# Cross attention on one core: the order of outputs, copies, statistics and last sums

## The chip, the cores and the metric

The kernel runs on one core of one Trainium2 chip. The metric is the device time of one execution in microseconds (us): 1736.73 us before the change, the median of three runs (1733.67 to 1740.61). The core's engines work side by side, each through a queue of its own in program order, and wait for each other on semaphores. TensorE (PE, with its weight loads as PEld) multiplies, VectorE (DVE) and ScalarE (ACT) evict, transpose and exponentiate, GpSimd (POOL) does small products and additions. DMAs are issued from the queues of ScalarE, POOL and SyncE (SP).

## The reference, cut to what matters

A decoder of four layers over x of shape (8, 56, 256): each layer is a self attention, a cross attention and a feed-forward block, each followed by a residual addition and a normalisation. The change touches the cross attentions of layers 0, 2 and 3, over a context `kv_c` of 1500 rows of 64 columns per batch element. They have 16 heads and differ in their weights (layer 3 leaves out the rotation of the queries):

```python
q_r = einsum("bshq,hqr->bhsr", q_big, W_qr)
k_r = einsum("bld,hdr->bhlr", kv_r, W_kr)        # kv_r: the rotated context
scores = einsum("bhsr,bhlr->bhsl", q_r, k_r)
attn = softmax(scores, axis=-1)
ctx_c = einsum("bhsl,bld->bhsd", attn, kv_r)
ctx_lat = einsum("bhsd,hkd->bhsk", ctx_c, w_kc_kv)
return ctx_lat.transpose(0, 2, 1, 3).reshape(B, S, H * K) @ Wo.T
...
x = layernorm(x + xattn(x, ctx_512, ...), axis=-1)
```

## The kernel before

The 448 rows of x lie as four tiles of 112 (`NT`, two batch elements each). `x_queries` folds the query weights so that a head's query against the context has 64 values; they lie in `qa`, on partitions 0 to 63 and again on 64 to 127. The two last projections are folded as well: per head `w_kc_kv` times `Wo` gives 64 x 256 numbers of `wm`. wm is made in four quarters of four heads by `weighted` (eight multiplications into columns 384 to 511 of the four banks `acc`, then one copy to `wm`).

`x_tiles` does the rest for the 8 batch elements. A batch has 16 x 56 = 896 queries, in 7 tiles of 128. One pass of the loop is a step n, for tile i = n mod 7 of batch b = n div 7; there are 56 steps. For a tile, `scored` multiplies 128 queries with 1500 keys into the four banks `sc4`, in two halves u; `moved` evicts each half on VectorE and keeps the row minimum of the negated scores; `weights` exponentiates on ScalarE and sums the rows; `turned` transposes 32 x 32 blocks on VectorE into `cells`. One batch later, in steps i = 0 to 5, `gather` multiplies the transposed weights with the context rows `kv`, into columns 0 to 223 of `acc`. `cells` is one buffer: the transposes of one batch write over what the sums of the batch before it have read, so a transpose of step i = 1 must wait for the sums of step i = 0.

The other parts of a batch are set into steps of the next ones. `inverted` takes the reciprocals of the row sums and puts them on diagonals (POOL); `spread` multiplies these with ones, so that each inverse stands on 64 partitions, in columns 256 to 383 of `acc`; `spread_out` copies them to `rec`. `halves_of(0)` at i = 5 and `halves_of(1)` at i = 6 copy the sums to `num` and `other`; `placed` adds the two and multiplies with the inverse on POOL into `qa`, whose first columns are free by then. `output` multiplies these with wm at i = 6, half a tile of rows (four of the eight pairs of heads) at a time, again into columns 384 to 511 of `acc`; `joined` copies that and adds it to X. In the first three batches, where there is nothing to output, step i = 6 has `weighted` in that place: quarters 2 and 3 in steps 13 and 20. Quarters 0 and 1 are made in steps 4 and 5, where no sums exist yet. `measured` takes mean and variance of a finished tile of X on VectorE: tiles 0 and 1 at i = 2 of batches 5 and 7, tile 2 behind the loop.

Every instruction of `x_tiles` goes through `do`, that is `ordered` (L361 to L374; the profile shows L365 for all of them). It binds each instruction to the one before it on its engine, so the queues keep the order in which the lines are written. The context rows of a batch come in thirds, four DMAs each, from ScalarE's queue (`rows_of`), the keys from POOL's queue (`columns`).

In the last step (n = 55) both halves of tile 2 are put out and joined. What is behind the loop (L1040 to L1066) is called the end here: the inverses of the last batch, its sums into `sc4`, the statistics and normalisation of tiles 0 to 2, the transposes of their rows (`turn_x`), the additions of the last sums' halves (`twin`, `last`) and the products with the inverse (`inv`) on VectorE, then the last tile's multiplication with wm, its addition, normalisation and transposes.

## Time and profile before

| | |
|---|---|
| median of three runs | 1736.73 us |
| profiled execution | 1739.46 us, span 1737.2 us |
| mean granted TensorE clock | 0.905 |
| PE, DVE, ACT, POOL busy | 1541.5, 1092.3, 622.5, 323.5 us |
| 168 exponentials on ACT | 1544 ns each |
| 168 transposes on DVE | 1766 ns each |
| evictions of a half on DVE | 935 and 958 ns |
| copies of a quarter of wm on ACT | 12, 585 ns each |
| copies of half an output (`y`) on ACT | 18, 372 ns each |
| the loops and ends of the three cross attentions | near 229 to 462, 878 to 1114, 1422 to 1657 us |

A line of the timeline reads: start in us from the span's start, duration in us, engine, source line, operation, output<-input, shapes (partitions x elements), count; in brackets the idle time of the engine just before and what ended it. A row can hold several instructions that follow each other. TensorE's fp32 multiplications show as two records each, so eight of them are x16. The view of busy time by window has, after the engines, the granted TensorE clock (1.00 is full), the busy share of the DMA engines and GB/s.

### The profile page before, as it was taken

The numbers are of one execution on the slowest core, as the hardware profiler recorded it, in microseconds if no ns is written. First come the engines' busy times: TensorE is split into PE (matmuls) and PEld (weight loads), VectorE is DVE, ScalarE is ACT, GpSimd is POOL, SyncE is SP. The second block draws the span as 40 slices with busy tenths as digits, with TensorE's granted clock in tenths as the row PEclk, the third lists the DMA queues.
The fourth block names the chain that finished last, engine by engine and source line by source line (L and its number), as shares of the span: only waits on it lengthen the run. The fifth ranks groups of instructions, "written<-read, shape, count | busy, mean of one in ns | idle before, by whom it ended". The sixth has DMA issues, their size and how long they took to land.

```text
span 1737.2 us, 37606 instructions
## 1 busy us (share of the span) xinstructions
PE 1541.5 (89%) x16308; PEld 939.0 (54%) x16308; DVE 1092.3 (63%) x1781; ACT 622.5 (36%) x906; POOL 323.5 (19%) x302
## 2 busy tenths in 40 slices
PE   7989979999878669978979999899988878999898
PEld 4666435555544335645425555665656834555656
DVE  1673579999476764254579999335462129999633
ACT  2421245565222232121235555322441034565421
POOL 4701511221122010021511211100230000221200
PEclk9988979999997889998979999797997677999989
DMA  8524422322120101122422322021210552222100
GB/s 320 182 73 127 119 54 85 96 84 72 30 84 13 38 25 29 43 82 94 122 66 82 97 84 72 15 79 48 62 44 12 158 127 59 75 84 81 51 1 11
DMA packets 52007, 133.74 MB, mean 77 GB/s; under 512 B 20785, under 2 KB 21249, under 8 KB 51842
## 3 DMA queue, kind: packets, MB, share of 16 engines
q1 hardware_dynamic: 19826, 65.36, 11.9%
q10 hardware_dynamic: 28368, 50.25, 10.3%
q0 software_dynamic: 3648, 15.73, 2.7%
q8 instruction: 128, 2.10, 0.5%
q14 instruction: 37, 0.30, 0.1%
HBM read 119.06 MB, written 6.75 MB: 72 GB/s over the span
## 4 chain that ended last, share of the span: by engine, by line
PE 53%; DVE 8%; issue 4%; ACT 3%; ACTq 1%; POOL 0%; DVEq 0%; POOLq 0%
PE ps_x L365 20%; PE ps_glu L357 8%; PE ps_y L357 7%; PE ps_qk L1617 2%; PE ps_v L1617 2%; PE ps_qh L357 2%; PE ps_m L357 2%; DVE sc L365 1%; PE ps_big L357 1%; PE ps_wqk L357 1%; PE ps_y L1617 1%; ACTq L365 1%; PE ps_qk L365 1%; PE ps_q L357 1%; PE ps_low L357 1%
## 5 line engine op out<-in xcount | busy, mean ns | idle before, releaser
L365 PE MATMUL ps_x<-kvT,qa 64*128 64x375 f32 x1344 | 306.0, 560 | 39.0 <-DVE sc L365 32.9
L365 ACT ACTIVATE sc<-sc,tops 128x1500 f32<-128x1500 f32 x168 | 259.3, 1544 | 144.6 <-DVE sc L365 113.9
L365 DVE STREAM_TRANSPOSE eT<-sc 128x1536 f32<-128x1536 f32 x168 | 296.7, 1766 | 21.5 <-ACT sc L365 12.4
L365 PE MATMUL ps_x<-eT,kv 32*64 32x224 f32 x9024 | 256.7, 357 | 2.2 <-issue 2.0
L365 PEld LDWEIGHTS ps_x<-eT,kv 32*64 32x64 f32 x9024 | 197.8, 133 | 67.2 <-issue 58.5
L365 PEld LDWEIGHTS ps_x<-kvT,qa 64*128 64x128 f32 x1344 | 113.0, 198 | 193.1 <-DVE sc L365 162.8
L365 DVE TENSOR_SCALAR_CACHE_REDUCE sc<-ps_x 128x750 f32<-128x750 f32 x168 | 157.1, 935 | 39.7 <-PE ps_x L365 39.6
L365 DVE TENSOR_SCALAR_CACHE_REDUCE sc<-ps_x,tops 128x750 f32<-128x750 f32 x168 | 160.9, 958 | 1.0 <-PE ps_x L365 0.5
L365 POOL TENSOR_TENSOR eT<-eyes,sums 128x224 f32<-128x224 f32 x24 | 13.3, 554 | 456.7 <-DVE sums L365 456.7
L780 POOL TENSOR_TENSOR rope<-rope,turn 96x448 f32<-96x448 f32 x64 | 70.9, 1129 | 88.8 <-DVE turn L778 88.8
L365 PE MATMUL ps_x<-wm,qa 128*112 128x128 f32 (+1 forms) x336 | 55.1, 326 | 18.9 <-DVE qa L365 11.9
L777 DVE TENSOR_TENSOR rope<-ps_big,consts 96x896 f32<-96x896 f32 x32 | 34.8, 1086 | 58.7 <-PE ps_big L357 58.7
L1133 ACT ACTIVATE act<-ps_glu 128x448 f32<-128x448 f32 (+1 forms) x52 | 28.2, 543 | 111.4 <-PE ps_glu L357 108.1
L1137 DVE TENSOR_TENSOR act<-ps_glu,act 128x448 f32<-128x448 f32 x43 | 26.8, 624 | 65.2 <-ACT act L1133 65.1
L613 DVE RECIPROCAL rec<-rec 128x896 f32<-128x896 f32 x8 | 46.0, 5753 | 28.8 <-ACT rec L612 28.8
L365 PEld LDWEIGHTS ps_x<-wm,qa 128*112 128x112 f32 x336 | 47.4, 200 | 30.6 <-issue 12.5
L407 ACT ACTIVATE rstd<-rstd 112x3 f32<-112x3 f32 (+2 forms) x21 | 4.3, 204 | 157.1 <-DVE rstd L406 156.9
L439 DVE TENSOR_TENSOR X<-X,ps_y 112x256 f32<-112x256 f32 x32 | 13.5, 422 | 69.8 <-PE ps_y L357 69.8
L1684 POOL TENSOR_TENSOR qk<-qk,sw 128x896 f32<-128x896 f32 x16 | 33.3, 2082 | 103.7 <-DVE sw L1683 103.7
L723 ACT COPY qa<-ps_qk 64x448 f32<-64x448 f32 x48 | 25.3, 526 | 68.6 <-PE ps_qk L365 46.8
L365 POOL TENSOR_TENSOR qa<-num,rec 64x448 f32<-64x448 f32 x42 | 47.8, 1138 | 2.9
L767 ACT COPY qh<-ps_qh 128x448 f32<-128x448 f32 x32 | 17.0, 532 | 64.9 <-PE ps_qh L357 64.9
(411 smaller groups left out, 2502.7 us busy)
## 6 DMA issues: line engine op xcount, KB each, us to landing
kv<-kv ACTq DMA_DIRECT2D x288, 128.0 KB, 2.7
kvT<-kvT POOLq DMA_DIRECT2D x24, 384.0 KB, 3.5
qa<-qa ACTq DMA_DIRECT2D x24, 224.0 KB, 3.7
raw<-in_ctx ACTq DMA_DIRECT2D x6, 512.0 KB, 5.1
kv<-raw POOLq DMA_DIRECT2D x6, 512.0 KB, 4.8
kvT<-by POOLq DMA_DIRECT2D x6, 512.0 KB, 4.4
l0a_q<-in_l0a_q SPq DMA_DIRECT2D x4, 512.0 KB, 10.5
l0a_c<-in_l0a_c SPq DMA_DIRECT2D x4, 512.0 KB, 9.0
```

Source lines behind the costliest of these rows:

```text
L357: ins = self.nc.tensor.matmul(out, lhsT, rhs, start=n == 0, stop=n == len(terms) - 1)
L365: call(*args, **kw)
L439: nc.vector.tensor_tensor(X[:, t, :], X[:, t, :], ps[:TT, :D], ALU.add)
L613: nc.vector.reciprocal(rec, rec)
L723: nc.scalar.copy(flat[rows, :, odd, h // 2 * S : (h // 2 + 1) * S], by_batch(ps[rows, :T]))
L767: nc.scalar.copy(qh, ps[:, :T])
L777: nc.vector.tensor_tensor(rope.rearrange("p a (b s) -> p a b s", b=NB), view, cos, ALU.mult)
L780: nc.gpsimd.tensor_tensor(rope[:, half, :], rope[:, half, :], turn[:, 1 - half, :], ALU.add)
L1133: nc.scalar.activation(act, ps[:m, 0, :T], AF.Silu)
L1137: nc.vector.tensor_tensor(act, ps[:m, 1, :T], act, ALU.mult)
L1617: tc.keep_in_program_order(nc.tensor.matmul(*args, **kw))
L1684: nc.gpsimd.tensor_tensor(qk, qk, sw, ALU.add)
```

## The change

There are five edits, all in `x_tiles`.

1. Quarters 0 and 1 of wm move from steps 4 and 5 to steps 0 and 1. The copy to `wm`, until now the end of `weighted`, is a function `kept`, called behind `weights(n + 1)` in all four steps.
2. The two `measured` in the loop go; all three stand behind the loop.
3. In the last step `halves_of(0)` moves from i = 5 to i = 6, behind the two outputs and `joined`.
4. `spread` of the last batch goes to `acc`, between the fourth and fifth of the last batch's six groups of sums, with `spread_out` right behind; before, it stood ahead of these sums and went to `sc4`, and its copy stood behind them.
5. The last sums are copied and added in two halves of the quarters (`quarters`): four copies and four additions of 64 x 256 in place of two and two of 64 x 512. Both products (`place`) follow them.

```diff
-            to = wm[:, 2 * quarter : 2 * quarter + 2, :].rearrange("p j (c n) -> p (j c) n", c=2)
+        def kept(quarter):
+            to = wm[:, 2 * quarter : 2 * quarter + 2, :].rearrange("p j (c n) -> p (j c) n", c=2)
             do(nc.scalar.copy, to, acc[:, :, 384:512])
...
-        def half_of(to, odd, swap, of=acc):
+        def half_of(to, odd, swap, of=acc, quarters=slice(0, 4)):
             mine, its = (slice(DC * o, DC * (o + 1)) for o in (odd, odd ^ swap))
-            do(nc.scalar.copy, by_query(to[mine]), by_quarter(of[its, :, 96 * odd : 96 * odd + 128]))
+            do(nc.scalar.copy, by_query(to[mine])[:, quarters], by_quarter(of[its, quarters, 96 * odd : 96 * odd + 128]))
...
-        end, wms = NB * NI, (4, 5, 13, 20)
+        end, wms = NB * NI, (0, 1, 13, 20)
...
-            if i == 2 and b >= 5 and b % 2:
-                measured((b - 5) // 2)
             turned(n)
             if n + 2 < end:
                 moved(n + 2, 1)
             if n + 1 < end:
                 weights(n + 1)
+            if n in wms:
+                kept(wms.index(n))
...
-                if i == 5:
+                if i == 5 and b < NB - 1:
                     halves_of(0)
                 if i == 6:
+                    if b == NB - 1:
+                        halves_of(0)
                     halves_of(1)
...
-        spread(b, sc4)
+        placed(b - 1)
         for j in range(NJ):
             gather(b, j, sc4)
-        placed(b - 1)
-        half_of(twin, 0, 1, sc4)
-        spread_out(inv, sc4)
-        half_of(twin, 1, 1, sc4)
-        measured(t - 1)
+            if j == 3:
+                spread(b)
+                spread_out(inv)
+        for k in range(t):
+            measured(k)
         self.norm(mv, range(t))
+        for quarters in (slice(0, 2), slice(2, 4)):
+            for odd in range(2):
+                half_of(twin, odd, 1, sc4, quarters)
+            for odd in range(2):
+                mine = slice(DC * odd, DC * (odd + 1))
+                a, c = (by_query(x[mine])[:, quarters] for x in (last, twin))
+                do(nc.vector.tensor_tensor, a, c, by_quarter(sc4[mine, quarters, 96 * odd : 96 * odd + 128]), ALU.add)
+        for odd in range(2):
+            place(b, nc.vector, odd, last, inv)
         self.turn_x(range(t), acc[:, 0:2])
-        for odd in range(2):
-            mine = slice(DC * odd, DC * (odd + 1))
-            do(
-                nc.vector.tensor_tensor, by_query(last[mine]), by_query(twin[mine]),
-                by_quarter(sc4[mine, :, 96 * odd : 96 * odd + 128]), ALU.add,
-            )
-            place(b, nc.vector, odd, last, inv)
```

More of the change, by code (lines that the diff above doesn't have):

```diff
@@ L919, in inverted, with spread @@
             )
-        def spread(b, to=acc):
+        def spread(b):
             diag = diags.pop(b)
@@ L928, in spread @@
                     pe(
-                        to[odd * DC : (odd + 1) * DC, i, 256:384], self.ones[rows, :DC],
+                        acc[odd * DC : (odd + 1) * DC, i, 256:384], self.ones[rows, :DC],
                         diag[rows, 3 * odd : 3 * odd + 4, :].rearrange("p t x -> p (t x)"), start=True, stop=True,
@@ L937, in by_quarter, with spread_out @@
             return a.rearrange("p i (t x) -> p i t x", x=32)
-        def spread_out(rec=rec, of=acc):
-            do(nc.scalar.copy, by_query(rec), by_quarter(of[:, :, 256:384]))
-        def half_of(to, odd, swap, of=acc):
+        def spread_out(rec=rec):
+            do(nc.scalar.copy, by_query(rec), by_quarter(acc[:, :, 256:384]))
+        def half_of(to, odd, swap, of=acc, quarters=slice(0, 4)):
             mine, its = (slice(DC * o, DC * (o + 1)) for o in (odd, odd ^ swap))
-            do(nc.scalar.copy, by_query(to[mine]), by_quarter(of[its, :, 96 * odd : 96 * odd + 128]))
+            do(nc.scalar.copy, by_query(to[mine])[:, quarters], by_quarter(of[its, quarters, 96 * odd : 96 * odd + 128]))
         def halves_of(odd):
```

## The prediction

> **What bounds the kernel now.** I read the page's busy shares first, then the three cross attentions (they fill 229 to 462, 878 to 1114 and 1422 to 1657 us) in the timeline, transpose by transpose, then their ends and the granted clock by microsecond. "Last layer" is the one from 1422 us.

> ```profile
> PE 1541.5 (89%) x16308; PEld 939.0 (54%) x16308; DVE 1092.3 (63%) x1781; ACT 622.5 (36%) x906; POOL 323.5 (19%) x302
> ```

> The average hides it: inside a cross attention VectorE sets the beat. Each step is two evictions and one 1.77 us transpose, and from start of transpose to start of transpose it takes 3.44 us in nearly every step of all three layers (3.39 at the first tile of a batch). Only steps that miss this beat, and the ends, can give time.

> The timeline at step 4, where the first quarter of wm is made:

> ```profile
> 1445.38 1.83 PE L365 MATMUL ps_x<-l3x_o,l3x_v 128*64 128x128 f32 x16
> ...
> 1447.26 0.59 ACT L365 COPY wm<-ps_x 128x512 f32<-128x512 f32 x1 [6.44 <-PE ps_x L365]
> 1447.74 1.55 ACT L365 ACTIVATE sc<-sc,tops 128x1500 f32<-128x1500 f32 x1
> ...
> 1449.41 1.78 DVE L365 STREAM_TRANSPOSE eT<-sc 128x1536 f32<-128x1536 f32 x1 [2.58 <-ACT sc L365]
> ```

> The copy stands ahead of the exponential in ScalarE's queue, waits for TensorE, and the transpose waits 2.58 us for the exponential. Step 13 does the same on a smaller scale, and so does step 20:

> ```profile
> 1480.99 0.58 ACT L365 COPY wm<-ps_x 128x512 f32<-128x512 f32 x1 [1.61 <-PE ps_x L365]
> ...
> 1481.47 1.55 ACT L365 ACTIVATE sc<-sc,tops 128x1500 f32<-128x1500 f32 x1
> ...
> 1483.14 1.78 DVE L365 STREAM_TRANSPOSE eT<-sc 128x1536 f32<-128x1536 f32 x1 [0.71 <-ACT sc L365]
> ```

> A statistic in the loop simply stands in VectorE's way:

> ```profile
> 1613.86 0.42 DVE L365 BATCH_NORM_STATS2 st<-X 112x6 f32<-112x256 f32 x1
> ...
> 1614.31 0.18 DVE L365 BATCH_NORM_AGGREGATE mv<-st 112x2 f32<-112x6 f32 x1
> 1614.41 1.76 DVE L365 STREAM_TRANSPOSE eT<-sc 128x1536 f32<-128x1536 f32 x1
> ```

> At the end TensorE is the chain:

> ```profile
> 1621.39 3.28 PE L365 MATMUL ps_x<-eT,kv 32*64 32x224 f32 x120
> ...
> 1626.16 0.58 ACT L365 COPY other<-ps_x 64x512 f32<-64x512 f32 x1
> ...
> 1626.88 5.39 PE L365 MATMUL ps_x<-wm,qa 128*112 128x128 f32 x32 [2.21 <-ACT other L365]
> ...
> 1632.47 8.82 PE L365 MATMUL ps_x<-eT,kv 32*64 32x224 f32 x339
> ...
> 1642.93 1.77 ACT L365 COPY sc<-ps_x 64x512 f32<-64x512 f32 x3 [7.23 <-PE ps_x L365]
> ...
> 1644.73 0.68 DVE L365 TENSOR_TENSOR sc<-sc,ps_x 64x512 f32<-64x512 f32 x1 [5.91 <-ACT sc L365]
> ```

> TensorE is free at 1624.67, waits 2.21 us for a copy of other data, and that hole also halves its clock (last column but two of the busy-by-window view):

> ```profile
> 1628.00:1629.00 1.00, 1.00 (x7) 1.00 (x6) 0.00 (x0) 0.00 (x0) 0.00 (x0) 0.50 0.00 0
> 1632.00:1633.00 1.00, 1.00 (x43) 0.86 (x49) 0.00 (x0) 0.62 (x2) 0.19 (x1) 1.00 0.00 0
> ```

> [...]

> **The change, part by part.** The reordered program keeps every multiplication; only the order on TensorE, ScalarE and VectorE changes, POOL's and SP's stay.

> *Copies of wm after the exponential; quarters 0 and 1 at steps 0 and 1.* The transpose of step 5 starts 5.83, 6.29 and 6.10 us after that of step 4; less 3.44 each, 7.90 us go. Steps 14 and 21 take 4.19 in all layers where 3.39 is the beat: 6 x 0.80 = 4.80. Price in the new place: after step 0's scores TensorE is idle from about 1430.6 to 1432.26; sixteen records take 1.15 us at full clock (the 1480 us quarter), so they fit. The copy (0.59) ends near 1432.3; the exponential behind it started at 1432.24, so it is 0.1 late, and its transpose comes only at 1436.42. Quarter 1 waits for copy 0 (same columns), is done near 1435.3, its copy near 1435.9 against an exponential at 1435.74: covered again. Without that cover (half clock: scores 2.87 of 3.44, plus 1.83) each of the two steps is 1.26 us over. Bounds 0 to 2.5 per layer; I take 0.25, 0.75 in all, since the layers start at full clock (1.00 at 1428 to 1432). A batch-start reads columns that `halves_of` must free; in steps 13 and 20 these copies now end about as before, with 0.25 us of slack in an undisturbed batch: I charge 0.4. Net 7.15 + 4.4 = 11.55. No DMA is moved here; buffers of the first wo tiles free some 14 us earlier, and SP's next loads (2.86 us at 1447.25) then fall near 1432 to 1437, where the DMA share is 0.00 to 0.02.

> *Statistics at the end.* Steps 37 and 51 take 3.99 to 4.00: 6 x 0.55 = 3.3 gained. At the end two pairs (0.43 + 0.18 each) fall into VectorE's 6.00 us idle ahead of the third pair: nothing. That cover gone, they'd cost 1.2 per layer.

> *Outputs before the copies.* They now wait for POOL's product of the batch before last alone, long done. They start at 1624.67. At full clock the two take 3.65 (first layer, 431.57 to 435.22), so to 1628.32; the last transpose is in by 1627.57. The sums follow (1632.47 to 1642.87, 10.40), with the spread of the inverses inside them (0.27): end 1638.99, 3.88 earlier. Second attention: 1081.72 + 3.65 + 10.15 + 0.27 = 1095.79 against 1099.67, 3.88. First: 428.96 + 3.65 + 10.26 + 0.27 = 443.14 against 445.75, 2.61 (its outputs ran warm already). Sum 10.4. What is late next? The last third of kv: its four DMAs stand on ScalarE's queue behind the second y copy, issued from 1632.43 and landed by 1636 (DMA share 0.03). Now four copies stand before them instead of two, but y comes at 1628.4: landed by 1632.0, or 1634.7 if all four copies must first finish; needed at 1635.7. The normalisation (table load after the four copies, near 1631.1, 1.28; then 3.33 from square root to last tile) ends near 1635.8, its transposes are due at 1639. Covered.

> *Last sums by two quarters.* Before: three copies 1.77, two adds and two products, 4.69 from end of sums to the last multiplication. The inverse's copy (0.58) moves under the sums. Half-size copies and adds aren't in the trace: bounds are half (0.29, 0.34) and all (0.58, 0.68) of the whole ones; I take the 112x256 rows, 0.37 and 0.42. Two copies 0.80, four adds to 2.56, two products 1.3, 0.15 to TensorE: 4.0. Gain 0.69 a layer, 2.1 (from -1.5 a layer to +1.1 at the bounds).

> *Clock.* Step 15 of the last layer lost 1.66 to half clock after a hole of 1480.96 to 1484.44, which mostly closes: I count 0.7. Elsewhere clock phases may fall either way: 0.

> Sum 11.55 + 3.3 + 10.4 + 2.1 + 0.7 = 28. The profiled execution's 1739.46 (span 1737.2) becomes 1711.5; it stands 2.7 above the median of 1736.73, so I predict 1708.7.

> **Rivals.** Main case, gain 24 to 33: 0.62.
> Half clock at the new places: outputs at 5.39 cost 1.74 x 3 = 5.2 and the first steps 6.75 more: gain 16, 1720.7. For it: these steps lie beside half-clock stretches. Against: the hole before the outputs closes. 0.16.
> TensorE takes back VectorE's time at batch starts: step 8 already loses 1.67 to 2.34 in each layer at half clock; if steps 15 and 22 do too (five new places by 2.0) the gain is 18, 1718.7. Against: steps 15 and 22 were mostly on the beat even after the stall. 0.09.
> Slower: half clock at every batch start, 21 places, 17 of them new, 34 us: 1742.7. It decides from 14 new places on. Against: from step 28 the trace has 1.00 and no miss. 0.03.
> No change: the steps wait for kv loads instead, so the early time is hidden anyway, 1735 or so; but over a layer the DMA share is 0.25, and issues of kv loads have held up a transpose only twice, by 0.17 and 0.31 us. 0.04.
> Better: the last multiplication (5.24 to 5.95, about 3.4 of it at half clock) stays at full clock, 1.7 each: gain 33 to 36, 1702. 0.06.

> **The numbers.** About 0.5%, 8.7 us, is what a measurement can tell. Faster 0.62 + 0.16 + 0.09 + 0.06 = 0.93, same 0.04, slower 0.03. Range 1702 to 1720: the main case, the batch-start rival and part of the two beside it.

> **What the profile after would show.** Step 5 at 3.4 in all layers, 14 and 21 at 3.4, 37 and 51 at 3.44. Outputs right behind the batch-6 sums with no wait and clock 1.00; no wait of the last sums on kv. Sums to last multiplication near 4.0. I am wrong if steps 1 to 3 stretch (early quarters not covered), if step 8 loses well over 2.3, or if the last kv third makes the sums wait.

## The result and the profile after

The changed kernel takes 1706.59 us, the median of six runs (1700.99 to 1712.55), against 1736.2 us before (six runs, 1733.67 to 1740.61): ratio 0.9829, 95% interval 0.9805 to 0.9852. I had predicted 1708.7 (1702 to 1720). The profiled execution is the longest of the six: 1712.55 us, span 1710.3, 26.9 us less than the profiled one of before. Its granted TensorE clock is 0.908 (before 0.905).

The busy shares do not show where the time went: each engine does within about 5 us what it did.

```profile
PE 1539.1 (90%) x16308; PEld 933.9 (55%) x16308; DVE 1091.5 (64%) x1787; ACT 624.1 (36%) x912; POOL 323.9 (19%) x302
```

The steps show it. Here the timeline of the last layer where quarter 0 (step 0) and quarter 2 (step 13) are made:

```profile
1414.01 1.14 PE L365 MATMUL ps_x<-l3x_o,l3x_v 128*64 128x128 f32 x16
...
1415.19 0.58 ACT L365 COPY wm<-ps_x 128x512 f32<-128x512 f32 x1 [1.25 <-PE ps_x L365]
...
1415.74 1.55 ACT L365 ACTIVATE sc<-sc,tops 128x1500 f32<-128x1500 f32 x1
...
1416.48 1.77 DVE L365 STREAM_TRANSPOSE eT<-sc 128x1536 f32<-128x1536 f32 x1
...
1459.77 1.54 ACT L365 ACTIVATE sc<-sc,tops 128x1500 f32<-128x1500 f32 x1
...
1461.48 0.58 ACT L365 COPY wm<-ps_x 128x512 f32<-128x512 f32 x1
...
1462.84 1.77 DVE L365 STREAM_TRANSPOSE eT<-sc 128x1536 f32<-128x1536 f32 x1
```

In both steps the copy now falls into a stretch in which no exponential is due, and the transpose has no bracket: it follows VectorE's own work. Before, the transpose behind the first quarter waited 2.58 us and that of step 14 0.71.

The end of the last layer, TensorE and what it waits for:

```profile
1600.72 3.75 PE L365 MATMUL ps_x<-wm,qa 128*112 128x128 f32 x32
...
1604.39 5.88 PE L365 MATMUL ps_x<-eT,kv 32*64 32x224 f32 x227
...
1615.43 1.51 ACT L365 COPY sc<-ps_x 64x256 f32<-64x256 f32 x4 [3.10 <-PE ps_x L365]
...
1616.20 1.75 DVE L365 TENSOR_TENSOR sc<-sc,ps_x 64x256 f32<-64x256 f32 x4 [4.12 <-ACT sc L365]
...
1617.98 1.27 DVE L365 TENSOR_TENSOR qa<-sc 64x448 f32<-64x448 f32 x2
...
1619.40 6.45 PE L365 MATMUL ps_x<-wm,qa 128*112 128x256 f32 x16 [3.28 <-DVE qa L365]
```

The outputs have no wait and take 3.75 us (before: a wait of 2.21 and 5.39). From the end of the sums to the last multiplication it is 4.0 us. But that multiplication itself takes 6.45 us, where it took 5.37 before:

```profile
1647.56 5.37 PE L365 MATMUL ps_x<-wm,qa 128*112 128x256 f32 x16 [3.97 <-DVE qa L365]
```

Start of transpose to start of transpose, in us (step 5 is the way from transpose 4 to transpose 5), for the steps that moved by more than half a microsecond in some layer. Steps 1 to 4 take 3.44 or 3.45 in all layers, before and after:

| step | first layer, before → after | second | last |
|---|---|---|---|
| 5 | 5.83 → 3.44 | 6.29 → 3.44 | 6.10 → 3.44 |
| 8 | 5.11 → 5.77 | 5.78 → 4.60 | 5.26 → 4.92 |
| 14 and 21, each | 4.19 → 3.39 | 4.19 → 3.40 | 4.19 → 3.40 |
| 15 | 3.44 → 3.44 | 3.44 → 3.44 | 5.11 → 3.44 |
| 16 | 3.45 → 4.58 | 3.44 → 3.44 | 3.44 → 3.44 |
| 37 and 51, each | 4.00 → 3.44 | 4.00 → 3.44 | 4.00 → 3.44 |
| 39 | 3.44 → 3.44 | 3.44 → 4.24 | 3.44 → 3.44 |
| transpose 0 to transpose 55 | 195.09 → 191.77 | 197.31 → 191.49 | 196.29 → 188.97 |
| transpose 55 to last multiplication | 19.94 → 16.12 | 21.48 → 16.35 | 21.73 → 17.39 |
| last multiplication | 5.24 → 6.53 | 5.95 → 5.37 | 5.37 → 6.45 |

The last three rows add up to −16.46, −13.29 and +1.79, together −28.0. The profiled executions differ by 26.9, so what lies outside these stretches became 1.1 us longer.

Two rows speak of TensorE's clock. Step 8 of the last layer in the timeline, and single microseconds from the view of busy time by window:

```profile
1439.76 2.16 PE L365 MATMUL ps_x<-eT,kv 32*64 32x224 f32 x64
...
1441.85 1.53 PE L365 MATMUL ps_x<-kvT,qa 64*128 64x375 f32 x8
1442.12 1.78 DVE L365 STREAM_TRANSPOSE eT<-sc 128x1536 f32<-128x1536 f32 x1 [1.40 <-PE ps_x L365]
```

```profile
1422.00:1423.00 1.00, 0.36 (x2) 0.30 (x4) 1.00 (x3) 0.32 (x1) 0.00 (x0) 1.00 0.00 0
...
1431.00:1432.00 1.00, 1.00 (x6) 0.28 (x2) 1.00 (x2) 0.20 (x2) 0.00 (x0) 0.50 0.00 0
...
1441.00:1442.00 1.00, 1.00 (x42) 0.63 (x28) 0.00 (x0) 0.60 (x2) 0.00 (x0) 1.00 0.00 0
...
1617.00:1618.00 1.00, 0.00 (x0) 0.00 (x0) 0.91 (x4) 0.68 (x1) 0.00 (x0) 1.00 0.00 0
...
1622.00:1623.00 1.00, 1.00 (x4) 0.69 (x3) 0.00 (x0) 0.00 (x0) 0.00 (x0) 0.50 0.00 0
```

In batch 0, where TensorE has little more than the scores, the clock falls to half at 1423.6 and stays there until 1440.7; the first sums of step 8 (2.16 us) then run late, and the transpose waits 1.40 us. In the hole ahead of the last multiplication it falls again, at 1618.2.

### The profile page after: what moved, and what is told of

It is laid out like the page before. It is cut to its first block, busy times and chain, and to the rows that moved or that the text cites. A ratio compares the mean times of both kernels' runs of the same rounds, so it can differ in the third digit from the quotient of the medians.

```text
span 1710.3 us, 37636 instructions
## 1 busy us (share of the span) xinstructions
PE 1539.1 (90%) x16308; PEld 933.9 (55%) x16308; DVE 1091.5 (64%) x1787; ACT 624.1 (36%) x912; POOL 323.9 (19%) x302
## 3 DMA queue, kind: packets, MB, share of 16 engines
HBM read 119.06 MB, written 6.75 MB: 74 GB/s over the span
## 4 chain that ended last, share of the span: by engine, by line
PE 50%; DVE 9%; issue 7%; ACT 2%; ACTq 1%; POOL 1%; DVEq 0%; POOLq 0%
PE ps_x L365 16%; PE ps_glu L357 8%; PE ps_y L357 7%; PE ps_qk L1624 2%; DVE sc L365 2%; PE ps_v L1624 2%; PE ps_m L357 2%; PE ps_qh L357 2%; PE ps_big L357 1%; PE ps_wqk L357 1%; PE ps_y L1624 1%; PE ps_q L357 1%; PE ps_qk L365 1%; ACTq L365 1%; PE ps_low L357 1%
## 5 line engine op out<-in xcount | busy, mean ns | idle before, releaser
L365 PE MATMUL ps_x<-kvT,qa 64*128 64x375 f32 x1344 | 308.0, 562 | 29.0 <-DVE sc L365 23.2
L365 ACT ACTIVATE sc<-sc,tops 128x1500 f32<-128x1500 f32 x168 | 259.2, 1544 | 148.4 <-DVE sc L365 113.0
L365 DVE STREAM_TRANSPOSE eT<-sc 128x1536 f32<-128x1536 f32 x168 | 296.9, 1768 | 9.1 <-PE ps_x L365 7.7
L365 PE MATMUL ps_x<-eT,kv 32*64 32x224 f32 x9024 | 255.3, 354 | 4.2 <-issue 4.2
L365 PEld LDWEIGHTS ps_x<-eT,kv 32*64 32x64 f32 x9024 | 196.2, 132 | 68.9 <-issue 60.6
L365 PEld LDWEIGHTS ps_x<-kvT,qa 64*128 64x128 f32 x1344 | 112.7, 199 | 186.1 <-DVE sc L365 160.8
L365 DVE TENSOR_SCALAR_CACHE_REDUCE sc<-ps_x 128x750 f32<-128x750 f32 x168 | 157.1, 935 | 38.1 <-PE ps_x L365 38.0
L365 DVE TENSOR_SCALAR_CACHE_REDUCE sc<-ps_x,tops 128x750 f32<-128x750 f32 x168 | 160.8, 957 | 1.0 <-PE ps_x L365 0.5
L365 POOL TENSOR_TENSOR eT<-eyes,sums 128x224 f32<-128x224 f32 x24 | 13.3, 554 | 449.2 <-DVE sums L365 449.2
L365 PE MATMUL ps_x<-wm,qa 128*112 128x128 f32 (+1 forms) x336 | 53.6, 318 | 9.0 <-DVE qa L365 9.0
L365 PEld LDWEIGHTS ps_x<-wm,qa 128*112 128x112 f32 x336 | 45.1, 191 | 21.2 <-issue 10.5
L365 POOL TENSOR_TENSOR qa<-num,rec 64x448 f32<-64x448 f32 x42 | 47.9, 1140 | 2.9
```

What stands on the lines that cost most here:

```text
L365: call(*args, **kw)
```

## The experiments

All the experiments but one start from the kernel after. Each is compared with the kernel before in ratio, and with the kernel after (0.9829) in its trace, step by step. An interval is about 0.2 to 0.3% to each side, 4 to 5 us, so single edits of 2 to 5 us are read from the trace and not from the medians. A trace is one execution only, and two things differ from trace to trace beside the edit: the phase of TensorE's clock, and stalls of TensorE that are told at the end (2.0 us in the trace of before, 4.2 in that of after).

### The order or the place of the copies

First, the copies ahead of the exponential again:

```diff
+            if n in wms:
+                kept(wms.index(n))
             if n + 1 < end:
                 weights(n + 1)
-            if n in wms:
-                kept(wms.index(n))
```

> The kernel after, with one thing undone: in steps 0, 1, 13 and 20 the copy of a quarter of wm stands ahead of the exponential of the next tile again (quarters 0 and 1 stay at steps 0 and 1). Theory (the stall came from the order in ScalarE's queue): steps 14 and 21 take 4.19 us again in all layers (6 x 0.80 = 4.8), and steps 1 and 2 stretch too, since the exponentials of the first steps then wait for TensorE: up to 1.2 per layer; 5 to 8 us more than the kernel after, so about 1712 to 1715. Rival (the place did it: at the old steps TensorE was at half clock, at the new ones it is not): steps 1 and 2 stay at 3.44 and 14 and 21 gain little or nothing from the order: within 2 us of the kernel after.

Measured: 1714.83 us, ratio 0.9877 (0.9857 to 0.9897), about 8 us more than after. Steps 14 and 21 take 4.19 in all layers. Step 1 takes 4.37, step 2 stays at 3.44. The loops (transpose 0 to 55) are 2.87, 2.87 and 2.30 us longer, 8.0 in all. The first stall in this kernel's timeline:

```profile
1417.67 0.58 ACT L365 COPY wm<-ps_x 128x512 f32<-128x512 f32 x1 [3.88 <-PE ps_x L365]
...
1418.15 1.55 ACT L365 ACTIVATE sc<-sc,tops 128x1500 f32<-128x1500 f32 x1
...
1419.89 1.78 DVE L365 STREAM_TRANSPOSE eT<-sc 128x1536 f32<-128x1536 f32 x1 [0.85 <-ACT sc L365]
```

The order is a cause: with the same place, and the quarter at the same speed (1.15 us here, 1.14 after), the stall is back.

Then the other half: the quarters at their old steps, the copies behind.

```diff
-        end, wms = NB * NI, (0, 1, 13, 20)
+        end, wms = NB * NI, (4, 5, 13, 20)
```

> The kernel after, with quarters 0 and 1 of wm back at steps 4 and 5; the copies stay behind the exponentials. Theory (the order is enough): step 5 takes 3.44 us or little more, and the time is that of the kernel after within 1.5 us. Rival (the place matters: at steps 4 and 5 TensorE is at half clock, scores 2.87 of 3.44 and a quarter 1.83, so 4.70 a step): steps 5 and 6 to 7 together lose 1.3 to 2.5 us a layer, 4 to 7.5 us more than the kernel after. In both cases step 8 shows whether the early quarters have cost it anything: 5.1 to 5.8 us if not.

Measured: 1703.01 us, ratio 0.9807 (0.9788 to 0.9827), not slower than after. Step 5 takes 3.44 in all layers, steps 6 and 7 stay on the beat, and step 8 takes 4.55, 4.55 and 3.44 where after has 5.77, 4.60 and 4.92. The loops are 1.58, 0.50 and 0.86 us shorter than after, 2.9 in all. The medians cannot tell 0.9807 from 0.9829; in this pair of traces the old place is a little better, and at step 8.

The third takes the kernel before and changes the order alone:

```diff
+        def kept(quarter):
             to = wm[:, 2 * quarter : 2 * quarter + 2, :].rearrange("p j (c n) -> p (j c) n", c=2)
             do(nc.scalar.copy, to, acc[:, :, 384:512])
...
             if n + 1 < end:
                 weights(n + 1)
+            if n in wms:
+                kept(wms.index(n))
```

> The kernel before, with one edit: the copy of a quarter of wm stands behind the exponential in steps 4, 5, 13 and 20 (the quarters stay where they were). Theory (the order in ScalarE's queue alone made the stalls of steps 5, 14 and 21): step 5 takes 3.44 and steps 14 and 21 take 3.39 us in all layers, 7.90 + 4.80 less what step 8 changes; about 12 to 15 us less than before, so 1721 to 1724, and the rest of the change's gain is that of the end and the statistics. Rival (moving the quarters did half of it): step 5 keeps 1.2 us or more a layer, at half clock; 8 us or less gained.

Measured: 1717.58 us, ratio 0.9897 (0.9877 to 0.9917), some 18 us less than before. The loops are 3.99, 5.88 and 6.26 us shorter, 16.1 in all. Step 4 of the last layer in its timeline, to be held against the 2.58 us of before:

```profile
1432.88 1.68 PE L365 MATMUL ps_x<-l3x_o,l3x_v 128*64 128x128 f32 x16
1434.24 1.77 DVE L365 STREAM_TRANSPOSE eT<-sc 128x1536 f32<-128x1536 f32 x1
1434.59 0.59 ACT L365 COPY wm<-ps_x 128x512 f32<-128x512 f32 x1 [2.84 <-PE ps_x L365]
1435.08 1.55 ACT L365 ACTIVATE sc<-sc,tops 128x1500 f32<-128x1500 f32 x1
...
1437.80 1.72 DVE L365 STREAM_TRANSPOSE eT<-sc 128x1536 f32<-128x1536 f32 x1
```

The quarter still takes 1.68 us (1.14 after; before 1.83, with the clock at 0.50 until 1446.88) and the copy still waits for it, but ScalarE has 1.8 us of idle time in an undisturbed step (busy for 1.64 of 3.44), and the copy now spends that. The gain is more than the 12.7 us of the stalls: step 8 gives another 2.5 over the three layers and step 15 of the last layer 1.67, while step 16 of the first takes 0.96 more. So the one edit of the order is worth more than half of the whole change, and no gain of the earlier place shows.

### Statistics

```diff
+            if i == 2 and b >= 5 and b % 2:
+                measured((b - 5) // 2)
             turned(n)
...
-        for k in range(t):
-            measured(k)
+        measured(t - 1)
```

> The kernel after, with the statistics of tiles 0 and 1 of X back in the loop (steps 37 and 51), that of tile 2 at the end. Theory: steps 37 and 51 take 3.99 to 4.00 us again, 6 x 0.55 = 3.3 us more; the end is not shorter, since VectorE is idle there anyway. So about 1710. Rival (VectorE's two statistics at the end delay the normalisation, which ends late): the end gets 1.2 us a layer shorter, and the time is that of the kernel after.

Measured: 1712.09 us, ratio 0.9856 (0.9836 to 0.9877). Steps 37 and 51 take 3.99 to 4.00 in all layers, 6 x 0.55 = 3.3 us. The loops are only 2.0 us longer, since other steps are shorter, about half of it step 39 of the second layer (3.63 against 4.24). Transpose 55 to the last multiplication is 16.13, 16.54 and 16.53 us (after: 16.12, 16.35, 17.39): the two statistics cost nothing in the first two ends. In the last one it is 0.86 shorter here; that this is due to the statistics is not shown, as the same stretch also takes 16.82 with the quarters at steps 4 and 5, where all the statistics are at the end.

### Outputs ahead of the copies

```diff
-                if i == 5 and b < NB - 1:
+                if i == 5:
                     halves_of(0)
                 if i == 6:
-                    if b == NB - 1:
-                        halves_of(0)
                     halves_of(1)
```

> The kernel after, with the copies of the first half of the last batch but one's sums (halves_of(0)) back in step 54, for the last batch too. Theory (the hole of TensorE ahead of the outputs and the clock that it halves): in the last step the outputs' y copies stand behind fewer copies, but the outputs must then wait only for the same data as before; if this order alone made the hole of 2.21 us, the hole is back and the two outputs take 5.39 instead of 3.75: 2.6 to 3.9 us a layer, 8 to 11 in all. Rival (the outputs waited for the product of the batch before last that stood behind the copies on POOL, or for columns that another edit freed): the outputs start at once as now, and nothing changes by more than 1 us; the gain is then from the other edits of the end.

Measured: 1715.53 us, ratio 0.9876 (0.9854 to 0.9898), about 9 us more than after. The timeline of the last layer:

```profile
1605.73 0.58 ACT L365 COPY other<-ps_x 64x512 f32<-64x512 f32 x1
...
1606.45 3.72 PE L365 MATMUL ps_x<-wm,qa 128*112 128x128 f32 x32 [2.21 <-ACT other L365]
```

The hole is back in all three layers (2.63, 2.21, 2.21), and with it 3.00, 2.51 and 2.35 us from transpose 55 to the last multiplication, 7.9 in all. So the order of the copies and the outputs made the wait, and the rival falls. But the outputs take 3.72 us in all three layers. The same hole that I had charged with half clock leaves it at full here. The view by window of the last layer, before (first two lines, hole from 1624.67 to 1626.88) and in this kernel (hole from 1604.24 to 1606.45); the first number behind the length is TensorE's busy time, the last but two the clock:

```profile
1624.38:1627.79 3.41, 1.20 (x16) 0.94 (x9) 3.12 (x3) 2.35 (x4) 0.56 (x1) 1.00 0.02 7
1627.79:1631.20 3.41, 3.41 (x18) 3.41 (x17) 0.00 (x0) 0.37 (x1) 0.72 (x1) 0.50 0.02 5
```

```profile
1604.76:1608.18 3.42, 1.73 (x16) 1.76 (x17) 3.21 (x7) 1.54 (x4) 0.56 (x1) 1.00 0.02 5
1608.18:1611.59 3.41, 3.41 (x83) 3.23 (x89) 0.21 (x2) 1.66 (x4) 1.45 (x2) 1.00 0.09 23
```

These stretches are single windows of the grid of 3.413 us on which the clock changes in the trace (see the end of the text). Before, the whole hole lies in one of them, and TensorE is busy for 0.35 of it; here it is cut in two, and the emptier window is still loaded 0.51.

### The last sums

The inverses spread ahead of the sums, their copy behind them:

```diff
         placed(b - 1)
+        spread(b, sc4)
         for j in range(NJ):
             gather(b, j, sc4)
-            if j == 3:
-                spread(b)
-                spread_out(inv)
...
         for quarters in (slice(0, 2), slice(2, 4)):
             for odd in range(2):
                 half_of(twin, odd, 1, sc4, quarters)
+            if quarters.start == 0:
+                spread_out(inv, sc4)
```

> The kernel after, with the inverses of the last batch spread ahead of the last sums into sc4 again, and their copy back between the copies behind the sums (after the first two of the four). Theory: the sums are no shorter, the whole copy of 0.58 us lies on the way from the sums to the last multiplication again, and the products wait for it: 0.6 us a layer, and the spread ahead of the sums must wait for the reciprocals and POOL's product behind the last transposes, up to 0.5 more: 1.5 to 3.5 us in all, so about 1709. Rival (the copies' place is hidden by VectorE's adds): 0 to 0.5 us a layer.

Measured: 1711.13 us, ratio 0.9856 (0.9829 to 0.9883). Timeline of its last layer:

```profile
1612.58 2.13 ACT L365 COPY sc<-ps_x 64x256 f32<-64x256 f32 x5 [6.39 <-PE ps_x L365]
...
1617.17 6.34 PE L365 MATMUL ps_x<-wm,qa 128*112 128x256 f32 x16 [3.89 <-DVE qa L365]
```

The fifth copy adds 0.62 to the row (2.13 against 1.51), and the idle time ahead of the last multiplication grows by 0.61 (3.89 against 3.28) in the first and the last layer. In the second it is 3.13 against 2.42. That is 1.9 us in all, as the theory had it. The copy of the inverses was on the way, and VectorE's additions do not hide it.

The other part, whole copies and additions:

```diff
-        for quarters in (slice(0, 2), slice(2, 4)):
+        for quarters in (slice(0, 4),):
```

> The kernel after, with the last sums copied and added whole (two copies and two additions of 64x512 in place of four and four of 64x256); all else as after. Theory from the rows 0.58 for a whole copy, 0.68 for a whole addition, 0.37 and 0.44 for half ones: sums to last multiplication is two copies, two additions, two products (1.16 + 0.68 x 2 less what overlaps + 1.27 + 0.15), 3.9 to 4.0 us against 4.0 now: the halves bring nothing, 0 to 0.3 us a layer either way, and the gain of the end was the copy that went under the sums. Rival (as I had predicted, splitting pays): 4.4 to 4.7 us, 0.4 to 0.7 a layer more.

```profile
1610.91 1.17 ACT L365 COPY sc<-ps_x 64x512 f32<-64x512 f32 x2 [3.40 <-PE ps_x L365]
...
1612.12 1.40 DVE L365 TENSOR_TENSOR sc<-sc,ps_x 64x512 f32<-64x512 f32 x2 [4.93 <-ACT sc L365]
...
1614.97 3.68 PE L365 MATMUL ps_x<-wm,qa 128*112 128x256 f32 x16 [3.39 <-DVE qa L365]
```

First copy to last multiplication is 4.06 us against 3.97 after: cutting in two is worth 0.1 us. VectorE starts 0.44 us earlier with the halves (0.77 behind the first copy against 1.21), but four additions take 1.75 where two take 1.40. The median is 1712.44 us, ratio 0.9874 (0.9849 to 0.9899), 6 us more than after (the two intervals just meet), and this trace does not explain it: the profiled execution took 1704.15 us, at clock 0.914, and the three other runs, 1712.26 to 1716.07, were granted 0.905 to 0.907.

### The clock

Two kernels add multiplications whose results nobody reads. The first fills the hole ahead of the last multiplication:

```diff
         self.turn_x(range(t), acc[:, 0:2])
+        for j in range(6):
+            pe(acc[:, 3, 0:256], self.ident, wm[:, j, :], start=True, stop=True)
```

> The kernel after, with six multiplications of 128x256 added on TensorE behind the transposes of the first three tiles, into columns that nothing reads, to keep it busy in the hole of 2.4 to 3.3 us before the last multiplication. Theory (the hole is what halves the clock of the last multiplication, 6.53, 5.37 and 6.45 us): it takes 3.4 to 4 us in all three layers, and the gain is 1 to 3 us a layer less what of the added work reaches past the hole (0 to 0.5): 3 to 7 us, so about 1701 to 1703. Rival A (its clock is halved whatever stands before it, by where the windows fall): 5.2 to 6.5 us again, time as after or up to 2 us more. Rival B (the added work runs at half clock and is in the way): the last multiplication starts 1 to 2 us later, slower than after.

Its timeline in the last layer, and the clock from the view by window:

```profile
1613.45 2.77 PE L365 MATMUL ps_x<-wm,consts 128*128 128x256 f32 x12
...
1615.29 1.27 DVE L365 TENSOR_TENSOR qa<-sc 64x448 f32<-64x448 f32 x2
1616.71 3.68 PE L365 MATMUL ps_x<-wm,qa 128*112 128x256 f32 x16 [0.49 <-DVE qa L365]
```

```profile
1617.00:1618.00 1.00, 1.00 (x6) 0.84 (x5) 0.00 (x0) 0.00 (x0) 0.00 (x0) 1.00 0.00 0
```

The last multiplication takes 3.68 us in all three layers, 7.3 us less than after (6.53 + 5.37 + 6.45 − 3 x 3.68), and the added work ends before the product that is waited for. Measured: 1703.26 us, ratio 0.9811 (0.9785 to 0.9837). The profiled execution is 8.3 us shorter than that of after; the medians differ by 3.3 us only, which these intervals do not tell from 7.

The second loads TensorE in batch 0, with a quarter of wm made again in steps 2 to 6:

```diff
             elif n in wms:
                 weighted(wms.index(n))
+            elif b == 0:
+                weighted(0, slice(0, 128))
```

> The kernel after, with the eight multiplications of a quarter of wm done again, into columns that nothing reads, in steps 2 to 6, where TensorE has only the scores to do. Theory (those steps' low load halves the clock, and step 8 pays for it with 4.60 to 5.77 us): the clock stays at 1.00 from step 1 on, step 8 takes 3.44, and the gain is 1.2 to 2.3 us a layer, 4 to 6 in all, so about 1701 to 1703. Rival (the clock falls all the same, and scores and added work take 4.7 of 3.44 us): steps 3 to 7 stretch to 4.7, 4 to 6 us a layer, 12 to 19 in all, slower than after.

Measured: 1700.76 us, ratio 0.9787 (0.9764 to 0.9811). The clock of the last layer is 1.00 from 1402 to 1445, from ahead of transpose 0 to behind transpose 8, and step 8 takes 3.44 in all layers. Its transpose in the last layer has no wait left:

```profile
1432.40 1.77 DVE L365 STREAM_TRANSPOSE eT<-sc 128x1536 f32<-128x1536 f32 x1
```

The loops are 3.70, 3.76 and 1.09 us shorter than after, 8.6 in all. Step 8 is 5.0 of it, as the theory had it. Another 3.1 are not the clock: step 16 of the first layer and step 23 of the second take 3.44 too (after: 4.58 and 5.44), because two stalls of TensorE that stood there, told at the end, are gone. From transpose 55 to the last multiplication it is 2.0 us longer than after. The last multiplication stays slow (6.42, 5.34, 6.71): there is nothing in its hole.

Both together:

> The kernel after with both additions: the multiplications of a quarter of wm done again, unread, in steps 2 to 6, and six unread multiplications of 128x256 ahead of the last multiplication. If the two are independent, step 8 takes 3.44 and the last multiplication 3.68 us in all layers: 8 us from the first and 7 to 8 from the second (1.69 to 2.85 a layer), about 1693 to 1696. Rival (the clock only changes its place: what is kept at full speed here falls elsewhere): 1699 or more, with new steps over 3.5 us between step 9 and the end.

Measured: 1695.57 us (1689.09 to 1702.69), ratio 0.9773 (0.9747 to 0.9799). Step 8 takes 3.44 and the last multiplication 3.68 in all layers. Some steps on the way are over the beat (step 46 of the first layer 3.92, step 25 between 3.64 and 3.74 in all three), but these sum to under 2 us. The way from transpose 55 to the last multiplication is longer than after by 1.81, 0.48 and 0.91 us; 1.9 of these 3.2 are more of the stalls told at the end. The time lies in the range for two independent additions, and both places take the times that they have at full clock.

Both, with half the load in batch 0 (`pairs=1`, four multiplications a step):

```diff
-        def weighted(quarter):
+        def weighted(quarter, cols=slice(384, 512), pairs=2):

-            for j in range(2):
+            for j in range(pairs):
...
             elif n in wms:
                 weighted(wms.index(n))
+            elif b == 0:
+                weighted(0, slice(0, 128), 1)
```

> As the kernel with both additions, but with half of them in steps 2 to 6 (four multiplications, 8 records, some 0.57 us a step at full clock, so that TensorE is busy for about 2.0 of 3.44 us where the full addition makes it 2.6 and none 1.44). If a load of six tenths is enough for the full clock: steps 2 to 8 as with the full addition, and the same time. Rival (it is not): half clock from some step between 4 and 6 on, scores and addition then take 4.0 of 3.44 us, steps 5 to 7 stretch and step 8 takes 4.6 to 5.8: 6 to 10 us more than with the full addition.

The addition in the timeline, and one step of batch 0, from transpose to transpose, in the view by window (after the length: busy time and records of each engine, then the clock):

```profile
1407.10 0.66 PE L365 MATMUL ps_x<-l3x_o,l3x_v 128*64 128x128 f32 x8
```

```profile
1409.57:1413.01 3.44, 2.35 (x18) 1.03 (x16) 3.44 (x6) 1.64 (x3) 0.00 (x0) 1.00 0.00 0
```

Measured: 1693.48 us (1691.22 to 1696.84), ratio 0.9768 (0.9747 to 0.9790), mean clock 0.934. The interval lies wholly under that of after: this version is better than both kernels. Step 8 takes 3.44 or 3.45 in all layers, so the smaller load is enough. That load is higher than the expectation said: by this row TensorE is busy for 2.35 of 3.44 us (0.68), against 1.76 (0.51) without and 2.83 (0.82) with the full addition.

## Why the prediction was right, and where it was not

**Copies of wm, the stalls.** Right in kind and size: step 5 lost exactly the 7.90 us and steps 14 and 21 the 6 x 0.80. The experiment with the copy ahead shows that the order in ScalarE's queue alone makes the stall (+8.0 us in the loops).

**The price of the new place.** Mis-sized. I charged 0.75 for the first steps and 0.4 for the batch starts; steps 1 to 4 cost nothing and the copies fit, but the loops are 2.9 us shorter with the old places, nearly all of it at step 8. That is one pair of traces: summed over the layers, step 8 takes 14.1 to 15.4 us in the seven kernels with the early quarters and nothing added in batch 0, and 12.5 and 13.6 in the two with the old places and the new order, so the price lies between 0.4 and 2.9. In the last layer of the kernel after with the old places, the clock is 0.50 until the first quarter is done and 1.00 from there through step 8 (in the other two step 8 takes 4.55); with the early places it is 1.00 in the first steps, where the scores leave slack, and 0.50 until step 8. That the clock is the cause, the added work in steps 2 to 6 shows: with it step 8 is on the beat (3.44 us, in the last layer at a clock of 1.00). I had looked for the price where the work went, and it stands where the work left.

**Statistics.** Right: 3.3 us predicted, 3.3 in the steps.

**Step 15.** I counted 0.7 for its clock; it gave 1.67 (5.11 to 3.44), with the order of the copies alone too. What I called a hole from 1480.96 to 1484.44 was none: the scores ran in it. The view by window has TensorE busy for 1.76 of the 3.41 us from 1481.02 to 1484.43, and half clock follows: a half load was enough.

**Outputs first.** The sum is right, one step of it was not. I predicted 10.4: a hole of 2.2 to 2.6 us in each layer and, in two of them, 1.74 us more for half clock, from the reading that "that hole also halves its clock". Undoing this edit alone brings the hole back (7.9 us) but not the half clock: outputs of 3.72 us in three layers of three. Before, two of three ran at 5.39, and with the order of the copies alone changed one of three (5.38 in the last layer). So a hole of 2.2 us can, but need not, halve the clock. In each of the traces of before and after all changes of the clock lie on one grid of 3.413 us, and the clock behind a hole went with the place of the hole on that grid: in both cases of half clock before, the outputs' hole lay in one window, loaded 0.35; at full clock, in the first layer before and in the last layer with this edit undone, it was cut in two, and the emptier window was loaded 0.46 and 0.51. In the kernel after, half clock followed holes of 2.42 and 3.28 us ahead of the last multiplication as well. The gain at half clock was real in this pair of profiles (twice 1.67 us), but it is not the edit's own.

**Last sums.** The size is right: 4.0 us to the last multiplication, as predicted. The inverses' copy is 0.6 of the 0.7 a layer, the cut in two 0.1. The single edits of the ends and the half clock of the outputs add up to the measured gain: 7.9 + 3.3 + 1.9 + 0.3 = 13.4, against 13.3.

**Last multiplication.** Missed. I counted 0 for the phases of the clock, and named full clock here as a better rival. It went the other way: 1.79 us lost in all. It is the same sixteen records; what changed is its phase against the clock. Before, half clock lasted one, two and one windows there, after two, one and two (from 443.99 to 450.82, 1089.11 to 1092.52 and 1618.18 to 1625.00). In these six cases half clock lasted one window where TensorE was busy for 0.92 or more of the first one, and two where it was busy for 0.69 or less.

**The sum.** 28 predicted and 28.0 by the last three rows of the table, 26.9 by the profiled executions, 29.6 by the medians. Part of this agreement is luck: the order of the copies 16.1 where I had 12.7 + 0.7, their place −2.9 instead of −1.15, statistics 3.3, the ends 13.3 instead of 12.5, the last multiplication −1.8 instead of 0. The 2.2 us by which TensorE's stalls told at the end grew were in no term.

**The rivals.** Half clock at the new places did not come: steps 1 to 4 took 3.44 in all three layers. TensorE did not take VectorE's time back at steps 15 and 22; step 8 of the first layer lost 0.66 more and those of the other layers less. The half clock at every batch start did not come (in the last layer the clock is 1.00 from 1440.7 to 1618.2). No step began to wait for kv in place of the removed wait; step 39 of the second layer was held up by the issue of kv's transfers, told below. Of my three signs of being wrong, none showed: steps 1 to 3 on the beat, step 8 at most 5.77 − 3.44 = 2.33, no wait of the last sums on kv.

## What to carry to other kernels

A copy that waits for a slower engine belongs behind the instruction that the critical engine waits for, as long as the queue has idle time to hold it (here 1.80 of 3.44 us). This one reordering, with the quarters at their old place, brought 16 us in the loops and about 18 in the medians. Where two stretches differ only in TensorE's clock, look at both places before explaining a difference: a load that is moved away can take the full clock with it (in the last layer step 8 took 3.44 us at a clock of 1.00 with the quarters at steps 4 and 5; with the quarters at 0 and 1 the clock was 0.50 until step 8, and it took 4.92). And a short hole ahead of dense multiplications on the critical path is worth filling with unread ones, if they end before the awaited data comes: here 3.68 in place of 5.4 to 6.5 us. Unread work at both places together took the median from 1706.59 to 1693.48.

## What the runs showed that I had not expected

```profile
1419.92:1423.36 3.44, 1.76 (x10) 0.60 (x8) 3.44 (x6) 1.64 (x3) 0.00 (x0) 1.00 0.39 135
...
1426.80:1430.25 3.45, 2.88 (x10) 1.13 (x8) 3.45 (x8) 1.65 (x3) 0.00 (x0) 0.50 0.00 0
```

The same scores load TensorE for 1.76 of 3.44 us at full clock, and a stretch of such work loses it at 1423.6. At half clock they load it for 2.88, and that stays at 0.50 for 17 us. With half the addition 2.35 of 3.44 us at full clock keep it at 1.00. So here a load of 0.68 held the full clock, and one of 0.84 at half clock did not win it back for 17 us.

- **The hole ahead of the last multiplication.** In eight kernels with a hole of 2.4 to 3.9 us there, 21 of 24 multiplications took 5.05 to 6.71 us and three 3.68; in the three kernels with the hole filled, to 0.3 to 0.7 us, nine of nine took 3.68. (In the kernel before and the one with the order alone, with 4.0 us, six of six took 5.18 to 5.95.)
- **The spread of one kernel's times goes with its clock.** Of the kernel after, the run of 1700.99 us has a mean clock of 0.917 and that of 1712.55 one of 0.908; with both additions 1689.09 at 0.938 and 1702.69 at 0.925. I read the runs of one kernel as so many draws of the phase; that nothing else differs between them is not shown.
- **DMA issue can hold up an exponential.** In step 39 of the second layer after, the four issues of a kv third took 2.99 us on ScalarE's queue, in its timeline:

```profile
1014.98 2.99 ACTq L365 DMA_DIRECT2D kv<-kv  x4
...
1018.07 1.54 ACT L365 ACTIVATE sc<-sc,tops 128x1500 f32<-128x1500 f32 x1 [2.53 <-DMA kv<-kv]
...
1019.74 1.78 DVE L365 STREAM_TRANSPOSE eT<-sc 128x1536 f32<-128x1536 f32 x1 [0.72 <-ACT sc L365]
```

Of the 72 groups of four such issues in this trace 51 take 1.72 to 1.77 us, the slowest 3.04. Why some are slower isn't known.

- **TensorE can stand still with nothing in the trace to wait for.** In step 16 of the first layer it did so for 1.13 us between two sums. Below the timeline stands the line of the page for the DMA queue "instruction" (packets, MB, share):

```profile
294.70 0.98 PE L365 MATMUL ps_x<-eT,kv 32*64 32x224 f32 x24 [1.13 <-issue]
...
295.81 1.78 DVE L365 STREAM_TRANSPOSE eT<-sc 128x1536 f32<-128x1536 f32 x1 [1.05 <-PE ps_x L365]
```

```profile
q8 instruction: 128, 2.10, 0.5%
```

That is 128 packets of 16384 bytes; TensorE has 32832 records in the trace (multiplications, weight loads and 216 of its sequencer). Number the records from 0 in order of time: all eight such stalls over 0.15 us in the cross attentions of before and after stand before a record whose number is 193 above a multiple of 256, and all end 1.32 to 1.54 us after the last packet of this queue landed. What TensorE waits for there is not shown, and no experiment was made for this alone. With the full load in batch 0 the stalls of step 16 and of step 23 of the second layer (1.98 us) are gone, and one of 0.85 stands in the first layer's end; with half of it one of 1.47 appears in step 23 of the first layer. In all they take 2.0 us before and 4.2 after. So instructions added on TensorE moved 1 to 2 us into a later step or out of it here.
